# One gather in sixteen of a graph layer replaced by single-column copies on ScalarE and VectorE

## The chip, the core and the metric

The kernel runs on one core of a Trainium2 chip. The metric is device microseconds of one launch. A core has five engines that run their own instruction streams in order: TensorE (PE in the profile, with PEld its weight loads), VectorE (DVE), ScalarE (ACT), GpSimd (POOL) and SyncE (SP), which here only issues DMAs. They meet at semaphores. SBUF and PSUM are on-chip memories of 128 partitions.

## The reference

One layer of message passing on a graph of 12,500 nodes with 64 features and 200,000 edges with 32 features. The edges are sorted by their destination.

```python
msg_in = concatenate([nodes[row], nodes[col], edge_features], axis=-1)   # row = src, col = dst
messages = relu(msg_in @ mW1 + mb1) @ mW2 + mb2                          # 160 -> 128 -> 64
aggregated = segment_sum(messages, col, num_segments=12500)
upd = relu(concatenate([nodes, aggregated]) @ uW1 + ub1) @ uW2 + ub2     # 128 -> 128 -> 64
out = layernorm(nodes + upd)
```

All of it is float32. The sources of the edges are random, so `nodes[row]` is a gather; the destinations rise, so the nodes of a few hundred edges lie close together.

## The kernel before

**Splitting the first layer.** The product with mW1 is split by its three inputs. `x @ mW1[0:64]` is computed once for all nodes into a table in DRAM, `tab_a` (L422), and `x @ mW1[64:128] + mb1` into `tab_b`. An edge then needs one row of `tab_a` (by its source), one of `tab_b` (by its destination) and a product of its 32 features.

**Tiles, groups and steps.** A tile is 128 edges. SUB = 8 tiles make one step s, SUP = 16 tiles make one group g, so a group is two steps; j = s % 2 tells which. There are 1563 tiles, 98 groups and 196 steps. The main loop (L583 to L622) writes out by hand what is issued in each step, and every engine takes its instructions in that order.

**The row gather.** `gather(s)` (L153) issues eight indirect DMAs on POOL, one for each tile: 128 rows of 512 bytes of `tab_a` into one of 14 row buffers. In the first XG = 8 steps rows of x are gathered in its place, and their product is made in `node_part`. A step's gathers are issued up to 13 steps ahead; `frees` (L145) tells which add must be done for the buffer to be free: the gathers of step s + 13, issued in step s, wait for the add of step s - 1.

**The edge product.** `edge_part(s)` (L242) makes eight matmuls of contraction 64 into PSUM tile `pc`. The weights are 32 rows of edge features and 32 rows of a one-hot matrix that picks the destination (L); the other operand is 32 rows of mW1 and a window of 32 rows of `tab_b` (rhs), which SP loads at an address read from a register (`windows`, L213). It is issued one step ahead: `edge_part(s + 1)` in step s. A float32 matmul shows as two pairs of weight load and matmul in the profile.

**Add and relu.** `node_part(s)` (L255) adds the gathered rows to `pc` on DVE (L272) and applies relu on ACT (L273), for all eight tiles at once. 

**The sum over edges.** `collect(s - 1)` in step s (L283) multiplies h by a one-hot selection of 32 slots for each tile (L298) into PSUM tile `sums`, and counts edges in `cnt` (L303). The selection is made by `select(g + 1)` in the even step of group g (L183): L190, L192 and L196 on DVE. Its buffer is one of two, so L196 waits for the `collect` of step s - 1. `counts` casts it on ACT (L204), in order behind it.

**Updates.** The destinations of some groups share one `sums` tile; 54 such updates follow one another over the run, each over fewer groups as the run goes on. With `due` an odd step: in the even step before it `close` copies the sums from PSUM on ACT (L317, L318), placed at the end of the step before this change; in the due step `update` makes the second layer's input (PE, L333, L334) and its relu (ACT, L336); in the even step after that `residual` makes the output and its statistics (PE L344, L345; DVE L349, L351; ACT square root L353); one step later `norm` scales (DVE L359, L362), first on DVE before that step's add, and `store` writes out. `columns` loads the x columns of the update's nodes.

**The start.** `chunk_a` makes `tab_a` in 13 chunks, with loads and stores on ACT's DMA queue, before the main loop. `rest(s)` spreads other loads and weight preparation over the first steps.

The order in the loop is: norm, windows, node_part, collect, select and load and counts (j = 0) or loadd (j = 1), a chunk of `tab_b`, edge_part of the next step, carry, update, residual, close, columns, rest, store.

Of the kernel before, what the change touches and what calls it, by code (L numbers as in the profile page):

```python
# [10 lines left out]
F32 = mybir.dt.float32  # L11
I32 = mybir.dt.int32
AF = mybir.ActivationFunctionType
ALU = mybir.AluOpType
# [3 lines left out]
P = 128  # L18
# [22 lines left out]
EARLY = NCH * P  # L41
GE = 20
BS = 8
UB = 3
NCOL = (-(-N // P) + UB) * P
UW = UB * P
# [16 lines left out]


@with_exitstack
def gnn_kernel(ctx: ExitStack, tc: tile.TileContext, x1T, x, eT, e_rows, src, dst, dst_row, wrow, wnext, whalf,
               mW1, mb1, mW2, mb2, uW1, ub1, uW2, ub2, out):

# [33 lines left out]
    past = const.tile([1, 1], F32, name="past")  # L104
    w1b = const.tile([P, DH], F32, name="w1b")
    b1 = const.tile([P, DH], F32, name="b1")

    sums_s = [const.tile([P, UW], F32, name=f"sums_s{k}") for k in range(2)]
    xw = [const.tile([P, UW], F32, name=f"xw{k}") for k in range(2)]
# [21 lines left out]
    cps = cpool.tile([P, WIN + SUP], F32, name="cps")  # L131
    slot = cps[:, :WIN]
    drc = const.tile([P, NT], F32, name="drc")
    flag_i = const.tile([1, 1], I32, name="flag_i")
    usup = const.tile([1, K], I32, name="usup")
    ustep = const.tile([1, K], I32, name="ustep")
# [4 lines left out]

    rows = ctx.enter_context(tc.tile_pool(name="rows", bufs=ROWB))
    xg = {}

    def frees(s):  # L145

# [3 lines left out]
    def tiles(s):  # L150
        return range(s * SUB, min((s + 1) * SUB, NT))

    def gather(s):  # L153

        if s >= XG or s % 2 == 0:
            buf = rows.tile([P, SUB, DH], F32, name="xg")
        else:
            buf = xg[s - 1][0]
        if s < XG:
            a = buf.rearrange("p k (b d) -> p (k b) d", d=D)[:, s % 2 * SUB:(s % 2 + 1) * SUB, :]  # L160
        else:
            a = buf.rearrange("p (b k) d -> p k b d", b=2)
        for i, t in enumerate(tiles(s)):
            nc.gpsimd.indirect_dma_start(  # L164
                out=a[:, i, :] if s < XG else a[:, i // 2, i % 2, :], out_offset=None, in_=A[:, :] if s >= XG else x[:, :],
                in_offset=bass.IndirectOffsetOnAxis(ap=src_s[:, t:t + 1], axis=0))
        xg[s] = buf, a

    with tc.tile_pool(name="sup", bufs=2) as sup, tc.tile_pool(name="work", bufs=2) as work, tc.manual_schedule():
# [31 lines left out]
        def counts(g):  # L201
            nt = min(SUP, NT - g * SUP)
            sb = sup.tile([P, SUP, WIN], BF, name="selb")
            nc.scalar.copy(sb[:, :nt], S[g][:, :nt])  # L204
            SB[g] = sb
# [27 lines left out]
            nc.scalar.copy(xt, pt)  # L233
            xs[s] = xt

        def parts(n):

            if n == SUB:
                return [slice(0, SUB)]
            return [slice(b * SUB // 2, b * SUB // 2 + (n - b + 1) // 2) for b in range(2) if n > b]  # L240

        def edge_part(s):  # L242

            n = len(tiles(s))
            g, j = divmod(s, SUP // SUB)
            pc = psum.tile([P, 2, SUB // 2, DH], F32, name="pc")
            for i in range(n):
                k, b = divmod(i, 2)
                q, m = 64 * b, j * SUB // 2 + k

                nc.tensor.matmul(pc[:, b, k, :], L[g][q:q + 64, m, :], rhs[g % 2][q:q + 64, m, :],  # L251
                                 start=s >= XG or k == 0, stop=s >= XG)
            pcs[s] = pc

        def node_part(s):  # L255

            n = len(tiles(s))
            pc = pcs.pop(s)
            h = work.tile([P, 2, SUB // 2, DH], F32, name="h")
            if s < XG:  # L260
                xt = xs.pop(s)
                for i in range(n):
                    k, b = divmod(i, 2)
                    q = 64 * b
                    nc.tensor.matmul(pc[:, b, k, :], xt[q:q + 64, k, :], w1a[q:q + 64], start=False,
                                     stop=i + 2 >= n)
                nc.scalar.activation(h, pc, AF.Relu)
            else:
                hf, pf = (t.rearrange("p b k f -> p (b k) f") for t in (h, pc))
                a = xg.pop(s)[0]  # L270
                for m in parts(n):
                    nc.vector.tensor_tensor(hf[:, m], pf[:, m], a[:, m], op=ALU.add)  # L272
                    nc.scalar.activation(hf[:, m], hf[:, m], AF.Relu)  # L273
            hs[s] = h

        def opened(u):
# [37 lines left out]
        def close(u):  # L314

            ps, pn = sums.pop(u)
            nc.scalar.copy(sums_s[u % 2], ps)  # L317
            nc.scalar.copy(xw[u % 2][0:1], pn)  # L318

        us = {}  # L320

# [46 lines left out]
            nc.sync.dma_start(out[bass.ds(n0, UW), :].rearrange("(c p) d -> p c d", p=P), o)  # L368


        WCH = 1024

        def relative(a, b):

# [19 lines left out]
        def columns_of(c, queue):  # L394

            xl = work.tile([P, HB * P], F32, name="xl")
            for h, m in spread(c):
                o = (c + HB * h) * P
                queue.dma_start(xl[64 * h:64 * h + 64, :m * P], x1T[1:, o:o + m * P])
            xls[c] = xl  # L400
# [82 lines left out]
        for k, c in enumerate(range(0, NB, NCH)):  # L483
            chunk_a(c)
            if k == 0:
                chunk_b(0, [B0v, Bv])
            if k == 2:

                w0 = wint[:, :GE * SUP]
                nc.vector.tensor_scalar(past, w0[:, GE * SUP - 1:], float(EARLY - WIN), None, op0=ALU.is_gt)  # L490
                nc.vector.tensor_scalar(w0, w0, float(EARLY - WIN), None, op0=ALU.min)
                windows(0)
                windows(1)
            if k == 4:
                relative(0, 8 * SUP)
            if k == 6:
                offsets()
            if k == 9:
                select(0)
                load(0)  # L500
                counts(0)
        columns_of(NCH, nc.sync)

        def rest(s):

            if s == 1:
                relative(8 * SUP, 8 * SUP + WCH)
            elif s == 2:
                relative(8 * SUP + WCH, NT)
                halves(4 * SUP, NTP // 2)  # L510
            elif s == BS:
                nc.sync.dma_start(wa, wrow.rearrange("o (p c) -> (o p) c", c=SUP))
                nc.sync.dma_start(wb, wnext.rearrange("o (p c) -> (o p) c", c=SUP))
                nc.scalar.dma_start(w2, mW2)
                nc.scalar.dma_start(u1a, uW1[D:2 * D, :])
                nc.scalar.dma_start(b2c, mb2.rearrange("(f o) -> f o", o=1))
                nc.vector.memset(uz[:D], 0.0)
                nc.vector.memset(ux[:D], 0.0)
                nc.vector.memset(eps, EPS)
                nc.vector.memset(ones, 1.0)  # L520
                nc.vector.tensor_copy(ux[D:], ident[D:, D:])
                nc.scalar.dma_start(uz[D:], uW1[0:D, :])
                nc.scalar.dma_start(ux[ONE:ONE + 1], ub2.rearrange("(o f) -> o f", o=1))
                nc.scalar.dma_start(ub1_s, ub1.rearrange("(f o) -> f o", o=1))
                nc.scalar.dma_start(u2, uW2)
            elif s == BS + 2:
                weights()
                checks()
# [54 lines left out]
        for s in range(last + 3):  # L583
            g, j = divmod(s, SUP // SUB)
            while gathered < NSUB and frees(gathered) < s:
                gather(gathered)
                gathered += 1
            if s - 2 in due:
                norm(due[s - 2])
            if s + 2 < NSUB:  # L590
                windows(s + 2)
            if s < NSUB:
                node_part(s)
            if 1 <= s <= NSUB:
                collect(s - 1)
            if j == 0 and g + 1 < NSUP:
                select(g + 1)
                load(g + 1)
                counts(g + 1)
            if j == 1 and g + 2 < NSUP:  # L600
                loadd(g + 2)
            if chunks and s >= BS and chunks[0] < NCH + NB * (s + 1 - BS) / (SUP // SUB * (GE - 1) - BS):
                if len(chunks) > 1:
                    columns_of(chunks[1], nc.sync)
                chunk_b(chunks.pop(0), [Bv])
            if s + 1 < NSUB:
                if s + 1 < XG:
                    transpose(s + 1)
                edge_part(s + 1)
            if s in due and due[s] + 1 < K:  # L610
                carry(due[s] + 1)
            if s in due:
                update(due[s])
            if s - 1 in due:
                residual(due[s - 1])
            if s + 1 in due:
                close(due[s + 1])
            if s + 2 in due:
                columns(due[s + 2])
            rest(s)  # L620
            if s - 2 in due:
                store(due[s - 2])  # L622
# [166 lines left out]
```

## Time and profile before

| what | value |
|---|---|
| median of three runs | 2792.62 us (2783.0 to 2799.24) |
| profiled execution, its time and span | 2797.45 us, 2795.7 us |
| PE, PEld busy | 1650.0 us (59%), 1427.7 us (51%) |
| POOL busy | 1476.6 us (53%) |
| DVE, ACT busy | 553.1 us (20%), 361.6 us (13%) |
| mean granted TensorE clock | 0.540 |
| indirect DMAs of `tab_a` and of x | 1499 and 64, 944 ns each |
| DMA engines' share; bytes moved | 0.2 to 0.3 in the main loop; 213.70 MB |

A row of the groups' view has the line, the engine, the operation, the tiles written and read, a count, busy time and the mean duration, then the idle time before these instructions and what ended it. "issue" is a wait for nothing that the profile shows, and "remote" one for something that the profile can't name. A timeline row has the start and duration in us, and in brackets the engine's idle time before it. Issuing of DMAs and register operations on an engine's sequencer are not counted as busy. [...]

In the main loop DVE and ACT each work a few microseconds in a step:

| row | engine | count | mean ns |
|---|---|---|---|
| L272 add | DVE | 189 | 1210 |
| L273 relu | ACT | 189 | 1047 |
| L190, L192, L196 selection | DVE | 84, 84 and 84 of the middle part | 220, 1221, 688 |
| L204 cast | ACT | 98 | 616 |
| L317, L318 close | ACT | 46 each of the middle part | 463, 462 |

### The profile page before, as it was taken

How to read it: one execution, taken by the hardware profiler on the slowest of the kernel's cores; microseconds unless marked ns; L12 is line 12 of the kernel's file. 1: busy time of each engine (PE TensorE's matmuls, PEld its weight loads, DVE VectorE, ACT ScalarE, POOL GpSimd, SP SyncE). 2: the span in 40 equal slices, each digit the busy share in tenths (PEclk: the TensorE clock that was granted, in tenths of full speed). 3: DMA queues.
4: the chain of work that ended last, by engine and by line, in shares of the span. 5: the costliest groups of instructions: out<-in, count | busy, mean ns of one | idle time of the engine just before them, and what ended most of it. 6: DMA issues, size and time to landing. Idle time of an engine off the chain costs nothing. (4 is left out here: it accounts for less than half of the span.)

```text
span 2795.7 us, 34750 instructions
## 1 busy us (share of the span) xinstructions
PE 1650.0 (59%) x9558; PEld 1427.7 (51%) x9558; DVE 553.1 (20%) x1103; ACT 361.6 (13%) x534; POOL 1476.6 (53%) x1572
## 2 busy tenths in 40 slices
PE   1412755555564646655656655656666676675788
PEld 1312654555454545544546544555555555564667
DVE  0200121222111112111211211212122222221233
ACT  0100101101010111111111111111111111111122
POOL 7175445654555655555555564565555555555510
PEclk6555555555555555555555555555555555555566
DMA  3531233333222222222222222222222222222221
GB/s 89 144 90 51 74 84 91 90 93 85 69 75 67 78 67 73 74 72 72 74 73 74 73 75 71 70 77 76 71 76 66 77 75 75 75 78 73 74 69 44
DMA packets 248063, 213.70 MB, mean 76 GB/s; under 512 B 81153, under 2 KB 213143, under 8 KB 247880
## 3 DMA queue, kind: packets, MB, share of 16 engines
q0 software_dynamic: 50016, 100.44, 14.0%
q1 hardware_dynamic: 182310, 100.72, 13.1%
q10 hardware_dynamic: 15554, 10.31, 1.3%
q8 instruction: 90, 1.47, 0.2%
q14 instruction: 93, 0.76, 0.1%
HBM read 192.55 MB, written 18.68 MB: 76 GB/s over the span
## 5 line engine op out<-in xcount | busy, mean ns | idle before, releaser
L164 POOL DMA_INDIRECT xg<-tab_a,src_s x1499 | 1415.0, 944 | 1183.8 <-DVE h L272 440.6
L251 PE MATMUL pc<-rhs,l 64*128 64x128 f32 x3126 | 531.4, 424 | 677.5 <-issue 411.8
L251 PEld LDWEIGHTS pc<-rhs,l 64*128 64x128 f32 x3126 | 432.1, 306 | 733.9 <-issue 629.4
L298 PEld LDWEIGHTS sums<-sel,h 128*128 128x128 f32 x3126 | 637.2, 301 | 206.6 <-issue 199.8
L298 PE MATMUL sums<-sel,h 128*128 128x32 f32 x3126 | 626.8, 366 | 151.7 <-issue 149.8
L272 DVE TENSOR_TENSOR h<-pc,xg 128x1024 f32<-128x1024 f32 x189 | 228.6, 1210 | 954.5 <-remote 319.5
L273 ACT ACTIVATE h<-h 128x1024 f32<-128x1024 f32 x189 | 197.7, 1047 | 598.9 <-DVE h L272 495.3
L196 DVE TENSOR_TENSOR sel<-cps,drc 128x512 f32<-128x512 f32 x98 | 67.3, 686 | 634.6 <-remote 333.4
L192 DVE TENSOR_TENSOR l<-l,cps 128x1024 f32<-128x1024 int32 (+1 forms) x101 | 123.3, 1221 | 206.0 <-DMA l<-in_dst_row 159.6
L204 ACT CAST selb<-sel 128x512 bf16<-128x512 f32 x98 | 60.4, 616 | 667.4 <-DVE sel L196 398.4
L303 PE MATMUL cnt<-selb,one 128*1 128x32 bf16 x1563 | 95.2, 188 | 51.0 <-issue 50.6
L336 ACT ACTIVATE hTu<-pu,ub_s 128x384 f32<-128x384 f32 x54 | 31.3, 580 | 696.0 <-remote 308.5
L344 PE MATMUL py<-ux,xw 128*128 128x64 f32 x324 | 95.5, 384 | 26.7 <-issue 23.1
L303 PEld LDWEIGHTS <-one 128*1 128x1 bf16 x1563 | 62.7, 83 | 89.7 <-issue 77.5
L345 PE MATMUL py<-u,hTu 128*128 128x64 f32 x324 | 93.9, 382 | 21.1 <-issue 20.7
L344 PEld LDWEIGHTS py<-ux,xw 128*128 128x128 f32 x324 | 77.1, 288 | 34.3 <-issue 28.4
L345 PEld LDWEIGHTS py<-u,hTu 128*128 128x128 f32 x324 | 79.8, 297 | 26.0 <-issue 25.5
L408 PE MATMUL pb<-w1a,xl 64*128 64x128 f32 x196 | 30.6, 430 | 99.6 <-DMA xl<-in_x1T 93.2
L333 PE MATMUL pu<-sums_s,w2u 128*128 128x384 f32 x108 | 88.2, 921 | 1.5 <-ACT sums_s L317 1.5
L408 PEld LDWEIGHTS pb<-w1a,xl 64*128 64x128 f32 x196 | 26.2, 311 | 103.7 <-issue 92.8
L334 PE MATMUL pu<-xw,uz 128*128 128x384 f32 x108 | 73.7, 782 | 0.0
L349 DVE BATCH_NORM_STATS2 st<-py 128x6 f32<-128x64 f32 x162 | 26.6, 220 | 237.6 <-PE py L345 120.3
(86 smaller groups left out, 594.3 us busy)
## 6 DMA issues: line engine op xcount, KB each, us to landing
l<-in_dst_row SPq DMA_DIRECT2D x196, 128.0 KB
l<-in_eT SPq DMA_DIRECT2D x196, 128.0 KB
rhs<-tab_b SPq DMA_DIRECT2D x1563, 16.0 KB
xg<-tab_a,src_s POOLq DMA_INDIRECT x1499
tab_b<-tb SPq DMA_DIRECT2D x13, 512.0 KB
tab_a<-tb ACTq DMA_DIRECT2D x12, 512.0 KB
xw<-in_x1T SPq DMA_DIRECT2D x54, 97.5 KB
out<-o SPq DMA_DIRECT2D x54, 96.0 KB
```

The source lines that it names most:

```text
L164: nc.gpsimd.indirect_dma_start(out=a[:, i, :] if s < XG else a[:, i // 2, i % 2, :], out_offset=None, in_=A[:, :] if s >= XG else x[:, :], ...
L192: nc.vector.tensor_tensor(l[r], l[r].bitcast(I32), node[r].unsqueeze(2).broadcast_to([r.stop - r.start, SUP // 2, P]), op=ALU.is_equal)
L196: nc.vector.tensor_tensor(s[:, :nt], slot.unsqueeze(1).broadcast_to([P, nt, WIN]), drc[:, g * SUP:g * SUP + nt].unsqueeze(2).broadcast_to( ...
L251: nc.tensor.matmul(pc[:, b, k, :], L[g][q:q + 64, m, :], rhs[g % 2][q:q + 64, m, :], start=s >= XG or k == 0, stop=s >= XG)
L272: nc.vector.tensor_tensor(hf[:, m], pf[:, m], a[:, m], op=ALU.add)
L273: nc.scalar.activation(hf[:, m], hf[:, m], AF.Relu)
L298: nc.tensor.matmul(ps[:, bass.ds(ws[i], WIN)], h[:, i % 2, i // 2, :], S[g][:, k0 + i, :], start=False, stop=ends and i == n - 1)
L303: nc.tensor.matmul(pn[:, bass.ds(ws[i], WIN)], one, SB[g][:, k0 + i, :], start=False, stop=ends and i == n - 1)
L333: nc.tensor.matmul(pu, w2u, sums_s[u % 2], start=True, stop=False)
L334: nc.tensor.matmul(pu, uz, xw[u % 2], start=False, stop=True)
L344: nc.tensor.matmul(py[:, i], xw[u % 2][:, i * P:(i + 1) * P], ux, start=True, stop=False)
L345: nc.tensor.matmul(py[:, i], hT[:, i * P:(i + 1) * P], u2, start=False, stop=True)
```

## The change

For one tile of each two groups (CG = 2 here counts steps of eight tiles: every second step, the odd ones, from step 13 on, where the step is full), the last tile of the step is no longer gathered. In its place its 128 x columns are put together on chip: x, transposed, is kept whole in SBUF (`xcol`, 64 partitions by 12,544 columns, loaded by SP in seven DMAs near the end of the table's making), and in each of two steps 64 columns are copied one by one into `xo` at addresses read from registers, 36 by ACT and 28 by DVE (`copies`). DVE does it as an addition of a zero that lies in PSUM. The sources of these tiles come from a small table `srow`, whose values are loaded into registers of ACT (twice 18) and DVE (28). A further matmul in `edge_part` multiplies `xo` by the weights `w1a` and adds to the tile's part of `pc`. In `node_part` the add covers seven tiles in such steps, and the last tile has a relu of its own straight from PSUM. `copies(s)` is called in each step behind the selection and the chunk of `tab_b` and ahead of the next `edge_part`; it works for the odd step two or three ahead.

Besides, `close` moves from the step's end to right behind `collect`, ahead of the selection and its cast.

```diff
+CG = 2
+CF = 6 * CG
+CA = 36
+NCT = -(-(NSUB - CF) // CG)
...
+    xcol = const.tile([P, NB * P], F32, name="xcol")
...
+    srow = const.tile([NCT, P], I32, name="srow")
+    xo = [const.tile([P, P], F32, name=f"xo{k}") for k in range(2)]
...
+    def copied(s):
+
+        return s >= CF and s % CG == CG - 1 and len(tiles(s)) == SUB
...
-        for i, t in enumerate(tiles(s)):
+        for i, t in enumerate(tiles(s)[:SUB - copied(s)]):
...
+                c = copied(s) and i == n - 1
                 nc.tensor.matmul(pc[:, b, k, :], L[g][q:q + 64, m, :], rhs[g % 2][q:q + 64, m, :],
-                                 start=s >= XG or k == 0, stop=s >= XG)
+                                 start=s >= XG or k == 0, stop=s >= XG and not c)
+                if c:
+                    nc.tensor.matmul(pc[:, b, k, :], xo[s // CG % 2][q:q + 64], w1a[q:q + 64], start=False, stop=True)
...
-                for m in parts(n):
+                for m in parts(n, copied(s)):
                     nc.vector.tensor_tensor(hf[:, m], pf[:, m], a[:, m], op=ALU.add)
                     nc.scalar.activation(hf[:, m], hf[:, m], AF.Relu)
+                if copied(s):
+                    nc.scalar.activation(h[:, 1, SUB // 2 - 1], pc[:, 1, SUB // 2 - 1], AF.Relu)
...
+        def copies(s):
+
+            t = (s + 2) // CG * CG + CG - 1
+            if t < CF or not t < NSUB or not copied(t):
+                return
+            n = P // CG
+            k = (s + 2) % CG * n
+            r = t // CG - CF // CG
+            to = xo[t // CG % 2]
+            def by_dve(o, i):
+                nc.vector.tensor_tensor(o, i, slot[D:, 0:1], op=ALU.add)
+
+            parts = []
+            for a, b, e, copy in ((k, k + CA // 2, ET.Activation, nc.scalar.copy),
+                                  (k + CA // 2, k + CA, ET.Activation, nc.scalar.copy),
+                                  (k + CA, k + n, ET.DVE, by_dve)):
+                _, v = nc.values_load_multi_w_load_instructions(
+                    srow[r:r + 1, a:b], engines=[e], min_val=0, max_val=N - 1,
+                    skip_runtime_bounds_check_because="sources are node numbers")
+                parts += [(copy, a + i, v[i]) for i in range(b - a)]
+            for copy, i, v in parts:
+                copy(to[D:, i:i + 1], xcol[D:, bass.ds(v, 1)])
...
+        XCH = 2048
...
+        def xload(c):
+
+            e = min(c + XCH, NB * P)
+            nc.sync.dma_start(xcol[D:, c:e], x1T[1:, c:e])
...
                 select(0)
                 load(0)
                 counts(0)
+                for c in range(0, NB * P, XCH):
+                    xload(c)
...
             elif s == 2:
+                nc.sync.dma_start(srow, src_row[CF * SUB + SUB * CG - 1::SUB * CG, :][:NCT])
...
             if 1 <= s <= NSUB:
                 collect(s - 1)
+            if s + 1 in due:
+                close(due[s + 1])
             if j == 0 and g + 1 < NSUP:
                 select(g + 1)
                 load(g + 1)
...
                 chunk_b(chunks.pop(0), [Bv])
+            copies(s)
...
                 residual(due[s - 1])
-            if s + 1 in due:
-                close(due[s + 1])
```

More of the change, by code (lines that the diff above doesn't have):

```diff
@@ L65, in gnn_kernel @@
 @with_exitstack
-def gnn_kernel(ctx: ExitStack, tc: tile.TileContext, x1T, x, eT, e_rows, src, dst, dst_row, wrow, wnext, whalf,
+def gnn_kernel(ctx: ExitStack, tc: tile.TileContext, x1T, x, eT, e_rows, src, src_row, dst, dst_row, wrow, wnext, whalf,
                mW1, mb1, mW2, mb2, uW1, ub1, uW2, ub2, out):
@@ L234, in transpose, with parts @@
             xs[s] = xt
-        def parts(n):
+        def parts(n, last=False):
             if n == SUB:
-                return [slice(0, SUB)]
+                return [slice(0, SUB - last)]
             return [slice(b * SUB // 2, b * SUB // 2 + (n - b + 1) // 2) for b in range(2) if n > b]
@@ L771 @@
         "src": sp.reshape(-1, P).T[:, :NT],
+        "src_row": sp.reshape(-1, P),
         "dst": dp[:EPAD].reshape(-1, P).T[:, :NT],
```

## The prediction

> **What bounds the kernel now.** I read the page's first part, then the waits, the timeline of one stretch, then each engine's rows there. No engine is full: PE 59%, POOL 53%. The waits (who waited, for whom, us in all, times, longest) say who holds whom:
>
> ```profile
> POOL xg L164 <- issue: 442.6, 1434, 1.0
> POOL xg L164 <- DVE h L272: 440.6, 67, 16.0
> ...
> POOL xg L164 <- DVE cps L190: 223.3, 50, 11.8
> ```
>
> A gather is 944 ns and 0.30 us of issue behind it, 1.25 us; eight are 10.0 us a step. POOL is idle 664 us more (second and third line), waiting for the add of L272, whose end frees a row buffer (the L190 behind it is named where it comes later). So DVE's adds start POOL's runs. From the add of step 11 (367.9 us, from the timeline) to that of step 182 (2687.2) a step takes 13.6 us: 10.0 of gathers, the rest mostly waits for an add. What delays the adds is seen in the timeline, here DVE's, then PE's and POOL's rows:
>
> ```profile
> 1498.47 1.22 DVE L272 TENSOR_TENSOR h<-pc,xg 128x1024 f32<-128x1024 f32 x1 [5.97 <-remote]
> 1499.61 0.22 DVE L190 TENSOR_SCALAR cps<-wh,pidx 128x8 f32<-128x8 int32 x1
> 1502.74 1.22 DVE L192 TENSOR_TENSOR l<-l,cps 128x1024 f32<-128x1024 int32 x1 [2.91 <-DMA l<-in_dst_row]
> 1515.51 0.69 DVE L196 TENSOR_TENSOR sel<-cps,drc 128x512 f32<-128x512 f32 x1 [11.55 <-remote]
> 1516.12 1.22 DVE L272 TENSOR_TENSOR h<-pc,xg 128x1024 f32<-128x1024 f32 x1
> ```
>
> ```profile
> 1504.16 0.37 PE L251 MATMUL pc<-rhs,l 64*128 64x128 f32 x1 [0.35 <-issue]
> 1505.59 0.37 PE L251 MATMUL pc<-rhs,l 64*128 64x128 f32 x1 [1.06 <-issue]
> ```
>
> ```profile
> 1511.49 0.94 POOL L164 DMA_INDIRECT xg<-tab_a,src_s  x1 [0.30 <-issue]
> 1517.60 0.94 POOL L164 DMA_INDIRECT xg<-tab_a,src_s  x1 [5.16 <-DVE h L272]
> ```
>
> While the rows of a run of gathers arrive, SP starts an instruction only each 0.70 us (or a multiple; 1503.43 to 1504.13 to 1504.85 here), and so does PE, once it has run some 80 more; PE's semaphores reach DVE late. Here the run ended at 1512.4 and the slow stretch at 1515.4, when selection and add went at once; 1.5 us later POOL had its next buffer. POOL's gap is 3.0 (tail) + 0.7 (L196) + 1.2 (L272) + 0.25 = 5.2 us. **What stands on DVE between the tail's end and the add stands in POOL's path.** DVE and ACT are not slowed in these stretches by what they do there now: up to 23 DVE instructions went at 0.1 us each.
>
> **What the change takes away.** One of 16 gathers in each odd step from 13 to 193: 91 x 1.25 = **-114 us**, if the gaps stay.
>
> **What it adds.** In each step 36 one-column copies on ACT and 28 on DVE, each with a register operation in front (PE has 3232 of these for its 3126 dynamic addresses), behind register loads (TENSOR_LOAD: 0.30 us for one value, 0.59 for eight, so an estimated 1.0 for 18 and 1.4 for 28; the sequencer does them while the engine waits or works, so I put them at nothing; uncovered on DVE they would cost 1.4 a step more). The trace has no such copy. Bounds. DVE: L351's small operations start 0.075 us apart, a whole L190 takes 0.22, so 2.1 to 6.2 us a step. I take L349's spacing, 0.135 us (three in 0.49; it too reads PSUM), plus a little for the register operation: 0.15, **4.2 us**. ACT, nearest row:
>
> ```profile
> 1921.58 0.30 ACT L353 ACTIVATE sd<-mv,eps 128x3 f32<-128x3 f32 x1 [3.20 <-DVE mv L351]
> 1921.78 0.46 ACT L317 COPY sums_s<-sums 128x384 f32<-128x384 f32 x1
> ```
>
> The next starts 0.203 us after a three-column operation: **7.3 us**. [...]
>
> **Where these lie.** In an even step they stand behind the selection of the next group (L190 to L196, on ACT the cast L204), before the next step's add, and before the residual's L349 to L353. I went through the timeline for all 86 even steps from 12 to 182:
> - In 33 of them L196 ended a wait and the add followed it with nothing between (as at 1515.51). The gathers cannot cover the copies: DVE's 4.2 us go in full between L196 and the add. 33 x 4.2 = **+141**.
> - In 46 a residual follows. An example, ACT's rows and then DVE's:
>
> ```profile
> 1536.06 0.62 ACT L204 CAST selb<-sel 128x512 bf16<-128x512 f32 x1 [4.55 <-issue]
> 1543.05 0.30 ACT L353 ACTIVATE sd<-mv,eps 128x3 f32<-128x3 f32 x1 [6.37 <-DVE mv L351]
> ```
>
> ```profile
> 1542.30 0.49 DVE L349 BATCH_NORM_STATS2 st<-py 128x6 f32<-128x64 f32 x3 [6.33 <-remote]
> 1542.71 0.30 DVE L351 BATCH_NORM_AGGREGATE mv<-st 128x2 f32<-128x6 f32 x3
> 1543.38 0.18 DVE L359 RECIPROCAL rs<-sd 128x3 f32<-128x3 f32 x1 [0.36 <-ACT sd L353]
> 1543.59 0.85 DVE L362 TENSOR_SCALAR o<-py,mv,rs 128x64 f32<-128x64 f32 x3
> 1544.35 1.21 DVE L272 TENSOR_TENSOR h<-pc,xg 128x1024 f32<-128x1024 f32 x1
> ```
>
> The add waits for the square root by way of L359 and L362. It is queued on ACT behind the copies, which end 0.7 + 7.3 = 8.0 us after L196; it now starts 0.75 behind L349, and L349 on average some 4 us after L196's end. Counted step by step, 42 are late, **+134** in all. Also queued behind ACT's copies: the next relu and, in a step that is due, hTu (L336); both mostly fall in a slow stretch, in which PE gets nowhere.
> - In the other even steps and in the odd ones the copies run beside POOL's run; in 12 odd steps DVE's idle time is under 4.2: **+22**.
>
> Together **+297**. [...]
>
> **End and start.** After the last gather (2681 us) two steps take 13.7 us, with some 4.4 of ACT (25.1 us in the last 96). With 2 x 7.3 more ACT needs 19.0: +5.3 for each of five pairs still copying, **+27**. At the start 3.2 MB of x columns go through SP's queue near 125 us, when queues move 200 to 260 GB/s; tab_a's last stores, which the gathers wait for, share that: **+8** (0 to 13; were they late altogether, the long first run at 138.6 us starts later). SP's issues for them, seven at about 0.4 us, stand before the windows of step 2, which wait for that first run anyway.
>
> **One answer each.** The new matmul is four short PE instructions in two steps; it waits for copies that were queued a step or more before, so I charge nothing; uncovered it would stop PE's queue, and the add behind it. The close moved ahead of the cast saves 0.6 us of ACT order; it and the cast wait for the same sums, so nothing (without the move it would stand behind 7.3 us of copies). The add over seven tiles saves an eighth of 1.22 us in each odd step, some 0.15 x 91 = 14 us at most, and the separate relu adds about 0.3 on ACT: together nothing. srow is one small DMA.
>
> **Sum.** -114 + 297 + 27 + 8 = +218. The profiled execution took 2797.45 us (span 2795.7), 4.8 over the median of the three runs, 2792.62. From it 3015 us; against the median about 3010. I forecast **3015 us**, the copies behind blocked selections; own range 2900 to 3160, chance 0.50.
>
> **Rivals.**
> - *Hidden, faster* (0.20): the later adds give PE and SP more clear time, selections come before the slow stretch, and all copies lie beside gathers: 2797 - 114 + 27 + 8 = **2718**. For it: the 8-gather runs, in which L196 went at 1535.29. Against it: PE's collect, which L196 waits for, comes behind an add and its relu (1.2 + 1.1 + 4 us), and SP is slow 1 to 3 us after the rows begin to come. With a copy at some 0.10 us on both engines and no tail it is near 2810.
> - *Throttled sequencers, slower still* (0.20): ACT and DVE, now with over 70 instructions a step, are held to one each 0.70 us like SP. Slow stretches fill some 8.6 us of a step (1580 us of SP's rows), room for 12 instructions, six copies. ACT's other 30 (6.0 us) and its 1.8 us of other work need clear time, where a step has about 5: 8.1 + 6.0 + 1.8 = 15.9 against 13.6, +2.3 x 171 = 393, with +35 for both ends **3225**, up to 3400 with waits behind it. For it: PE and SP. Against: DVE's 23.
> - *No change* (0.03): at the low prices, +85 or +147 against 114.
> - Between the last and the forecast's range: 0.07.
>
> Within 0.5% (14 us) is what a measurement cannot tell from no change. Faster 0.20, same 0.03, slower 0.77. The range 2700 to 3360 takes in the upper part of the first rival, leaves out the far end of the second, and holds the unknown prices.
>
> **What would show it.** Right: rows of 28 DVE copies between L196 and L272 where none stood, 0.15 us apart; ACT's 0.20 apart; POOL's wait for DVE up from 664 to near 950 us while its issues fall by 91. Wrong: a POOL gap of 5 us still behind blocked selections; copies at 0.08 us; copies 0.7 us apart in the runs (the throttle); or PE's new matmul waiting long for xo, which I put at nothing. If selections stop waiting, the first rival has it.

## The result, and the profile after

The changed kernel takes 2962.77 us (median of 4 runs, 2939.45 to 2982.32) where the kernel before, run beside it, takes 2795.93: a ratio of 1.0596, 95% interval 1.0504 to 1.0687. It is slower by 167 us. A second series of the same kernel, run later, gave 3006.05 (ratio 1.0775, 1.0685 to 1.0865), so the loss is 167 to 215 us.

The profiled execution has a span of 2955.8 us (2795.7 before). Its waits, in the same columns as those of before:

```profile
ACT xo L358 <- issue: 1328.7, 949, 6.4
POOL xg L176 <- DVE h L287: 665.3, 86, 18.7
DVE xo L347 <- issue: 637.4, 871, 1.8
POOL xg L176 <- issue: 409.2, 1291, 7.5
...
PE pc L267 <- ACT xo L358: 240.1, 40, 15.9
POOL xg L176 <- DVE cps L202: 226.2, 75, 4.0
...
DVE rs L399 <- ACT sd L393: 155.0, 54, 6.5
```

POOL's waits that name DVE rise from 664 to 892 us; its issue time falls with the 91 gathers. New are PE's wait for the copied columns and, largest of all, idle time of ACT ahead of copies that nothing in the profile explains ("issue"). L399's wait for the square root is 155 us, where the same wait was 17 before. From POOL's rows I made an account of the whole span. A run is a row of gathers that follow one another after 0.30 us; a gap is a pause of over 0.6 us between two runs. The last two columns belong to experiments below.

| us | before | after | no_copies | aligned |
|---|---|---|---|---|
| up to the first gather of `tab_a` | 138.6 | 148.3 | 146.7 | 145.4 |
| in runs | 1834.5 | 1708.9 | 1720.4 | 1704.7 |
| in gaps | 708.3 | 944.0 | 644.8 | 798.0 |
| after the last gather | 114.3 | 154.6 | 116.9 | 118.9 |
| span | 2795.7 | 2955.8 | 2628.8 | 2767.1 |

The runs are 126 us shorter, and the gaps 236 us longer. (Some 14 of the 126 only changed their place: there are 46 more gaps, and each holds 0.30 us that stood in a run.) What DVE does inside the gaps, summed from its rows (what is left of the gaps is smaller work):

| us inside POOL's gaps | before | after | aligned |
|---|---|---|---|
| column copies | 0 | 115 | 75 |
| idle, then a copy | 0 | 143 | 98 |
| idle, then L399 (waits for the square root) | 13 | 127 | 52 |
| the add itself | 142 | 190 | 192 |
| idle, then the add | 183 | 144 | 162 |
| idle, then the selection L208 | 138 | 69 | 51 |
| idle, then the statistics L389 | 90 | 14 | 34 |

Of the 143 us ahead of copies 53 stand before the first copy of a step and 90 between copies. One gap of 15.7 us shows most of this. The timeline of the changed kernel, POOL's rows, then DVE's, then ACT's (start, duration, and in brackets the idle time before):

```profile
1577.40 0.94 POOL L176 DMA_INDIRECT xg<-tab_a,src_s  x1 [0.30 <-issue]
1594.05 0.94 POOL L176 DMA_INDIRECT xg<-tab_a,src_s  x1 [15.71 <-DVE h L287]
```

```profile
1580.14 0.69 DVE L208 TENSOR_TENSOR sel<-cps,drc 128x512 f32<-128x512 f32 x1 [10.38 <-remote]
1582.23 0.42 DVE L347 TENSOR_TENSOR xo<-xcol,cps 64x1 f32<-64x1 f32 x3 [1.40 <-issue]
1582.97 3.25 DVE L347 TENSOR_TENSOR xo<-xcol,cps 64x1 f32<-64x1 f32 x25 [0.32 <-issue]
1586.25 0.50 DVE L389 BATCH_NORM_STATS2 st<-py 128x6 f32<-128x64 f32 x3
1586.78 0.32 DVE L391 BATCH_NORM_AGGREGATE mv<-st 128x2 f32<-128x6 f32 x3
1591.72 0.18 DVE L399 RECIPROCAL rs<-sd 128x3 f32<-128x3 f32 x1 [4.62 <-ACT sd L393]
1591.93 0.85 DVE L402 TENSOR_SCALAR o<-py,mv,rs 128x64 f32<-128x64 f32 x3
1592.70 1.08 DVE L287 TENSOR_TENSOR h<-pc,xg 128x896 f32<-128x896 f32 x1
```

```profile
1583.21 0.61 ACT L216 CAST selb<-sel 128x512 bf16<-128x512 f32 x1
1587.37 2.92 ACT L358 COPY xo<-xcol 64x1 f32 x28 [3.55 <-issue]
1590.48 0.89 ACT L358 COPY xo<-xcol 64x1 f32 x8 [0.19 <-issue]
1591.39 0.30 ACT L393 ACTIVATE sd<-mv,eps 128x3 f32<-128x3 f32 x1
```

The 28 DVE copies stand between L208 and L287, as forecast. The square root L393 stands behind ACT's 36 copies, as forecast. But the copies of ACT take 4.0 us here, not 7.3, and 3.55 us before them ACT does nothing. DVE has 1.40 of the same. The views of line L353, where the registers are loaded, give the reason (count, then shortest, median and longest in ns):

```profile
L353 ACTq TENSOR_LOAD <-srow x364: 746/2759/5341, 355.1 to 2909.3; - x182
L353 DVEq TENSOR_LOAD <-srow x182: 1847/1896/2157, 355.2 to 2906.0; - x182
```

ACT's median mixes two kinds: in nearly every step its first load takes about 1.50 us and its second about 4.00 (medians), though both bring 18 values. In the gap above the second runs from 1583.29 to 1587.21, and the first copy starts at 1587.37. What makes the second slower is the question of the last two experiments.

The 0.70-us stretches, too, now reach the copies. ACT's rows in another step of the same timeline:

```profile
1537.17 1.84 ACT L358 COPY xo<-xcol 64x1 f32 x15 [4.57 <-issue]
...
1550.44 0.19 ACT L358 COPY xo<-xcol 64x1 f32 x1 [1.19 <-issue]
1551.18 0.19 ACT L358 COPY xo<-xcol 64x1 f32 x1 [0.55 <-issue]
1552.57 0.19 ACT L358 COPY xo<-xcol 64x1 f32 x1 [1.20 <-issue]
1553.32 0.29 ACT L358 COPY xo<-xcol 64x1 f32 x2 [0.56 <-issue]
```

```profile
1553.65 0.79 PE L267 MATMUL pc<-w1a,xo 64*128 64x128 f32 x2 [15.19 <-ACT xo L358]
```

Single copies start 0.74, 1.39 and 0.75 us apart here, and PE, whose new matmul waits for the last of them, stands for 15.19 us. In the whole run 630 of ACT's 6370 intervals from copy to copy are 0.6 us or longer (610 us in all), and 573 of DVE's 4914 (557 us).

### The profile page after: what moved, and what is told of

Its sections match the earlier page's. It is cut to its first block, busy times and chain, and to the rows that moved or that the text cites. A ratio compares the mean times of both kernels' runs of the same rounds, so it can differ in the third digit from the quotient of the medians.

```text
span 2955.8 us, 58846 instructions
## 1 busy us (share of the span) xinstructions
PE 1634.4 (55%) x9740; PEld 1417.7 (48%) x9740; DVE 1231.8 (42%) x6199; ACT 1106.8 (37%) x7177; POOL 1393.7 (47%) x1481
## 5 line engine op out<-in xcount | busy, mean ns | idle before, releaser
L176 POOL DMA_INDIRECT xg<-tab_a,src_s x1408 | 1332.0, 946 | 1386.4 <-DVE h L287 665.3
L358 ACT COPY xo<-xcol 64x1 f32 x6552 | 746.8, 188 | 1330.6 <-issue 1328.7
L347 DVE TENSOR_TENSOR xo<-xcol,cps 64x1 f32<-64x1 f32 x5096 | 684.6, 159 | 640.9 <-issue 637.4
L315 PEld LDWEIGHTS sums<-sel,h 128*128 128x128 f32 x3126 | 655.6, 313 | 171.2 <-issue 118.9
L264 PE MATMUL pc<-rhs,l 64*128 64x128 f32 x3126 | 432.7, 426 | 481.5 <-DVE o L402 171.9
L264 PEld LDWEIGHTS pc<-rhs,l 64*128 64x128 f32 x3126 | 363.3, 314 | 507.5 <-DVE o L402 189.5
L287 DVE TENSOR_TENSOR h<-pc,xg 128x1024 f32<-128x1024 f32 (+1 forms) x189 | 217.0, 1148 | 314.6 <-DMA xg<-tab_a,src_s 137.4
L288 ACT ACTIVATE h<-h 128x1024 f32<-128x1024 f32 (+1 forms) x189 | 187.9, 995 | 137.8 <-DVE h L287 132.8
L208 DVE TENSOR_TENSOR sel<-cps,drc 128x512 f32<-128x512 f32 x98 | 67.2, 685 | 385.2 <-remote 208.1
L267 PE MATMUL pc<-w1a,xo 64*128 64x128 f32 x182 | 64.3, 454 | 280.5 <-ACT xo L358 240.1
L267 PEld LDWEIGHTS pc<-w1a,xo 64*128 64x128 f32 x182 | 46.1, 311 | 303.6 <-ACT xo L358 260.8
L373 PE MATMUL pu<-sums_s,w2u 128*128 128x384 f32 x108 | 88.2, 920 | 146.7 <-DVE h L287 70.3
L373 PEld LDWEIGHTS pu<-sums_s,w2u 128*128 128x128 f32 x108 | 26.9, 309 | 156.2 <-DVE h L287 73.3
L384 PEld LDWEIGHTS py<-ux,xw 128*128 128x128 f32 x324 | 82.9, 313 | 15.7 <-ACT hTu L376 7.3
```

What stands on the lines that cost most here:

```text
L176: nc.gpsimd.indirect_dma_start(out=a[:, i, :] if s < XG else a[:, i // 2, i % 2, :], out_offset=None, in_=A[:, :] if s >= XG else x[:, :], ...
L315: nc.tensor.matmul(ps[:, bass.ds(ws[i], WIN)], h[:, i % 2, i // 2, :], S[g][:, k0 + i, :], start=False, stop=ends and i == n - 1)
L347: nc.vector.tensor_tensor(o, i, slot[D:, 0:1], op=ALU.add)
L358: copy(to[D:, i:i + 1], xcol[D:, bass.ds(v, 1)])
L373: nc.tensor.matmul(pu, w2u, sums_s[u % 2], start=True, stop=False)
L384: nc.tensor.matmul(py[:, i], xw[u % 2][:, i * P:(i + 1) * P], ux, start=True, stop=False)
```

## The experiments

Two theories stood at first. The **queue**: what stands on DVE ahead of the add, and on ACT ahead of the square root, is paid in POOL's gap. The **throttle**: ACT's added instructions fall into the 0.70-us stretches, and PE waits for `xo`. Register loads had a part in the queue theory alone: some 50 us on ACT and, taking nearly all idle time ahead of copies in the gaps for loads, 121 on DVE, where only 53 lie ahead of the first copy of a step. The first four runs take the change apart, and were made on one chip, beside a kernel before of 2789.22 us.

**No copies at all.** The gathers stay reduced, the matmul reads zeros, to which `xo` is set once at the start.

```diff
-            copies(s)
```

> The changed kernel without any copy and register load for one: xo is set to zero once, so the product of the last tile's x rows in each odd step is left out; gathers, the further matmul, the load of xcol and the moved close stay as changed. Theory Q (queue: copies and register loads stand on DVE and ACT ahead of the add that frees POOL): all of the loss goes, the gathers' gain stays, 2796 - 126 + 10 and perhaps less than 10 us of tail, 2680 to 2700 us. Theory T (throttle: copies at 0.70 us in the runs of gathers hold up PE's matmul with xo): the same 2680 to 2700. If it stays above 2760, the loss lies in something else, the matmul, the seven-tile add or xcol's load.

Measured 2623.95 us, ratio 0.9394 (0.9341 to 0.9447). The gathers and the rest of the change are worth 165 us, not 114. The account shows where the other 51 lie: the runs are 114 us shorter, the gaps 64, and start and end 11 longer. All that the copies and their loads cost is therefore some 340 us by the first series of the changed kernel, and 382 by the second, which ran on the same chip as this run. Both theories had the gain too small.

**DVE's 28 copies alone**, the other columns left at zero in the same way.

```diff
-            for a, b, e, copy in ((k, k + CA // 2, ET.Activation, nc.scalar.copy),
-                                  (k + CA // 2, k + CA, ET.Activation, nc.scalar.copy),
-                                  (k + CA, k + n, ET.DVE, by_dve)):
+            for a, b, e, copy in ((k + CA, k + n, ET.DVE, by_dve),):
```

> Only DVE's 28 copies of a step and their load; ACT's 36 columns of xo stay zero, so a part of the last tile's product is left out. Theory Q: the square root is no longer behind ACT's copies (113 us of POOL's gaps in the changed kernel), DVE's copies (115) and its register loads (121) stay: 2830 to 2870 us, with rows of 28 copies and 1.7 us of idle time ahead of them still in POOL's gaps. Theory T: ACT's copies were the ones PE waited for (240 us), so with them gone most of the loss goes: 2700 to 2760.

Measured 2779.17 us, ratio 0.9968 (0.9946 to 0.9990): DVE's part costs 155 us over no copies. The value lies between the two ranges and favours neither.

**ACT's 36 copies alone**, in two loads of 18.

```diff
-                                  (k + CA // 2, k + CA, ET.Activation, nc.scalar.copy),
-                                  (k + CA, k + n, ET.DVE, by_dve)):
+                                  (k + CA // 2, k + CA, ET.Activation, nc.scalar.copy)):
```

> Only ACT's 36 copies of a step and their two loads; DVE's 28 columns of xo stay zero, so a part of the last tile's product is left out. Theory Q: DVE's copies and loads leave POOL's gaps (236 us), the wait of the reciprocal for the square root stays (some 110 us or a little more): 2730 to 2800 us. Theory T: PE's matmul still waits for ACT's copies, 240 us in the changed kernel: 2900 to 2960.

Measured 3166.34 us, ratio 1.1343 (1.1282 to 1.1405): slower than the whole change, with less work, and past both ranges. Its waits:

```profile
ACT xo L357 <- issue: 1551.7, 1261, 6.3
POOL xg L176 <- DVE h L287: 943.0, 85, 17.6
...
PE pc L267 <- ACT xo L357: 803.0, 85, 15.5
```

PE waits for `xo` in 85 steps, not 40. The profile shows 46 runs of 15 gathers here and 5 in the changed kernel. My reading is that in the long ones ACT comes to its copies in the midst of a 0.70-us stretch and PE's queue stands until the stretch ends, and that DVE's copies, by delaying adds, break these runs and give ACT clear time; no run has that alone. The two parts don't add up in any case (155 and 542 us over no copies, and some 340 or 382 for both), and PE's wait for ACT's copies grows from 240 to 803 us. What brings ACT to its copies so late was not yet known.

**The same copies from fixed columns**: no register loads and no register operations; the columns are the wrong ones.

```diff
-                _, v = nc.values_load_multi_w_load_instructions(
...
-                copy(to[D:, i:i + 1], xcol[D:, bass.ds(v, 1)])
+                parts += [(copy, a + i, 97 * (a + i)) for i in range(b - a)]
...
+                copy(to[D:, i:i + 1], xcol[D:, v:v + 1])
```

> All 64 copies of a step, but from fixed columns of xcol (97 times the place), so without register loads and without the register operation ahead of each copy; the last tile of the odd steps gets the wrong x rows. Theory Q: copies of 0.10 and 0.13 us stay in POOL's gaps (115 us, and the square root behind ACT's 3.6 us), the loads go (121 us on DVE, some 50 on ACT): 2770 to 2830 us. Theory T: half the instructions, so the copies are done before the slow stretch bites and no copy stands 0.70 us after another; if the throttle was the loss: 2700 to 2740.

Measured 2773.33 us, ratio 0.9936 (0.9915 to 0.9958). All 64 copies are there, and 190 us of the first series are gone, 233 of the second, which ran on the same chip. This is in the queue theory's range: the way to the addresses costs more than the copies, which keep some 150 us (2773 against 2624). ACT's longest idle time ahead of a copy falls from 6.4 to 1.2 us:

```profile
ACT xo L355 <- issue: 632.1, 906, 1.2
```

The throttle is still there, with 846 of ACT's intervals at 0.6 us or longer, where its theory had expected none. Copies now start 0.072 us apart on DVE in the clear and 0.091 on ACT, instead of 0.129 and 0.101, so 0.057 of the 0.129 us of a DVE copy went with its register operation. The run doesn't tell what the loads cost from what the register operations cost.

**Three runs on a chip without the stretches.** These and a fourth for reference ran on another chip, on which the kernel before takes 1984.47 us. There the 0.70-us stretches are missing: after the first 250 us 15 of SP's intervals are near 0.70 or 1.40 us in the kernel before with a third buffer, against 1610 in the kernel before on the other chip. POOL runs from its first gather to its last almost without a gap: in the kernel before with a third buffer 1469 of its waits are issue, none over 0.3 us, 447.8 us in all. The expectations had been put in numbers for the other kind of chip, so what they were to tell apart could not be told; and the changed kernel as it is was not run on this chip.

*The copies two steps earlier*, into one of three `xo`:

```diff
-            t = (s + 2) // CG * CG + CG - 1
+            t = (s + 4) // CG * CG + CG - 1
...
-            k = (s + 2) % CG * n
+            k = (s + 4) % CG * n
```

> All copies, worked two steps earlier (for the odd step four or five ahead) into three xo tiles, so that PE's matmul with xo comes at least two steps behind its copies. Theory T (ACT's copies at 0.70 us hold up PE at this matmul, and all behind it): PE's wait for xo (240 us in the changed kernel) goes and the add comes earlier: 2780 to 2870 us. Theory Q (DVE's copies and loads, and the square root behind ACT's copies, stand ahead of the add): these stay where they are, 2930 to 2980.

Measured 2076.8 us, ratio 1.0463 (1.0446 to 1.0481). Its waits:

```profile
ACT xo L358 <- issue: 758.5, 282, 5.7
...
DVE rs L399 <- ACT sd L393: 267.2, 54, 6.7
...
POOL xg L176 <- DVE h L287: 99.6, 31, 4.2
```

POOL hardly waits, and its last gather ends at 1933 us, yet 145 us follow it (26 in the kernel before with a third buffer). ACT needs 5.5 us of loads, 3.7 of copies and some 1.8 of other work in a step, about 11, where POOL needs 9.4: the consumers fall behind the gathers and finish later. No interval from copy to copy reaches 0.6 us here, and the loads alone are half of ACT's step.

*The copies behind the residual*:

```diff
-            copies(s)
             if s + 1 < NSUB:
...
                 residual(due[s - 1])
+            copies(s)
```

> The call of the copies moved behind update and residual in each step, so the statistics (L389, L391), the square root and hTu stand ahead of the copies on DVE and ACT. Theory Q: the reciprocal's wait for the square root in POOL's gaps (127 us, before the change 13) goes and the copies of a blocked step then stand behind the statistics: 2830 to 2900 us. Theory T: copies come later still and PE waits longer for xo: 2960 to 3050.

Measured 2370.65 us, ratio 1.1952 (1.1932 to 1.1972). PE's new matmul then waits 338 us for `xo` and the gaps are 348 us, against some 100 in the run before. On this chip it is the worst of the three.

*A third buffer for the selection and its kin*, in the changed kernel and in the kernel before:

```diff
-    with tc.tile_pool(name="sup", bufs=2) as sup, tc.tile_pool(name="work", bufs=2) as work, tc.manual_schedule():
+    with tc.tile_pool(name="sup", bufs=3) as sup, tc.tile_pool(name="work", bufs=2) as work, tc.manual_schedule():
```

> The changed kernel with three buffers for the selection and its cast in place of two, so L208 does not wait for the collect of the step before. Theory Q: no selection is blocked, the copies begin right behind the add beside POOL's run: the idle time ahead of sel (69 us) and much of xo and its loads (236) leave POOL's gaps: 2780 to 2860 us. Theory T: more copies fall into the slow stretches and PE waits more for xo: 2930 to 3050.

> The kernel before with three selection buffers. A blocked selection costs there only its own 0.7 us and the cast's order: 34 x 0.7 = 24 us less, 2760 to 2795 us, under either theory; under 2740 would mean that the waits of L196 cost more than DVE's own time behind them.

Measured 2084.63 us, ratio 1.0497 (1.0479 to 1.0516), and 1984.0 us, ratio 1.0000 (0.9991 to 1.0008). To the kernel before the third buffer is worth nothing on this chip. The change with it loses 5%; what the buffer does for the changed kernel itself can't be told without that kernel's time here.

**Half of it**, beside the changed kernel itself, again on a chip with the stretches (before 2791.45 us): one tile of each four groups, 18 copies on ACT in one load and 14 on DVE.

```diff
-CG = 2
+CG = 4
...
-CA = 36
+CA = 18
```

> Half of the change: one tile of each four groups (every fourth step) instead of each two, so about 45 gathers fewer instead of 91, and 18 copies on ACT (one load of 18 values) and 14 on DVE in each step; the close stays moved. Two cases, by the chip that this run meets. On a chip with 0.70-us stretches (kernel before near 2790 us): the theory 'what stands on DVE ahead of an add and on ACT ahead of the square root is paid in POOL's gap' has -165 x 45/91 = -82 us (from the run without copies) and about half of the register loads and copies in 34 to 50 blocked steps, some +90: 2770 to 2830, ratio 0.99 to 1.015. The rival 'a fixed number of copies falls into each slow stretch, so ACT only gets slow above some 50 instructions' has ACT's series unthrottled and no wait of PE for xo: 2700 to 2760, ratio 0.97 to 0.985. On a chip without such stretches (before near 1985 us): POOL's unbroken run is the bound, so -45 x 1.25 = -56 us and, with ACT's work in a step down from about 11 to 6 us, no long tail: 1925 to 1945, ratio 0.97 to 0.98; if instead the copies delay adds as on the other chip: 1985 or more.

> The changed kernel itself, unaltered, beside the others of this call. On a chip with 0.70-us stretches (before near 2790 us): ratio 1.05 to 1.07, 2930 to 2985 us. On a chip without them (before near 1985 us): no gap of POOL from copies ahead of an add, but ACT needs about 5.5 us of register loads, 3.7 of copies and 1.8 of other work, 11 us a step, where POOL needs 9.4, so the consumers fall behind and the work after the last gather grows to over 100 us: ratio 1.04 to 1.06, 2065 to 2105 us. If ACT's register loads cost nothing there, ACT has 5.5 us a step, no long tail, and the ratio is 0.945 to 0.96.

Half the change measured 2937.21 us, ratio 1.0510 (1.0453 to 1.0568), far above what either theory allowed; the whole one 3006.05, ratio 1.0775 (1.0685 to 1.0865). Half the change has two thirds of the loss (146 of 215 us). The loads of this kernel:

```profile
L352 ACTq TENSOR_LOAD <-srow x168: 700/1474/1729, 518.0 to 2881.1; - x168
L352 DVEq TENSOR_LOAD <-srow x168: 1034/3258/4291, 521.8 to 2879.7; - x168
```

DVE loads 14 values in 3.26 us, where 28 took 1.90. Ahead of an add stand now 3.26 + 1.84 = 5.1 us, against 1.90 + 3.65 = 5.55 for twice the columns. What the slow loads have in common is where they start: ACT's second 18 values at byte 72 of a step's share of a row, DVE's 14 at byte 72; the fast ones start at byte 0 or 144. That is the third theory, of the **misaligned load**: the start decides the time, at byte 72, which is no multiple of 16, 0.22 to 0.23 us a value, at 0 and 144 0.07 to 0.08. The last two runs test it, again on a chip with the stretches (before 2792.51 us).

**The changed kernel with ACT's loads as 20 and 16**, all else as it was:

```diff
+CA1 = 20
...
-            for a, b, e, copy in ((k, k + CA // 2, ET.Activation, nc.scalar.copy),
-                                  (k + CA // 2, k + CA, ET.Activation, nc.scalar.copy),
+            for a, b, e, copy in ((k, k + CA1, ET.Activation, nc.scalar.copy),
+                                  (k + CA1, k + CA, ET.Activation, nc.scalar.copy),
```

> The changed kernel with ACT's 36 values loaded as 20 and 16 instead of 18 and 18, nothing else changed. In all runs so far a load of 18 values that starts 72 bytes into its row took 4.04 us, one of 14 values at 72 bytes 3.26, while 18 values at byte 0 took 1.51 and 28 at byte 144 took 1.9. Theory A: a load whose start is not a multiple of 16 bytes costs about 0.23 us a value, an aligned one 0.07 to 0.08; so the load of 16 at byte 80 takes 1.2 to 1.4 us, ACT is 2.5 us a step shorter, the square root behind it is as much earlier in some 50 residual steps. On a chip with 0.70-us stretches (before near 2790 us): -125 from the changed kernel, 2830 to 2890 us, ratio 1.015 to 1.035. On a chip without them (before near 1985 us): ACT's 11 us a step become 8.5, less than POOL's 9.4, so the long tail goes and the 91 gathers show: 1870 to 1910, ratio 0.94 to 0.965. Rival: the second load of a step is slow whatever its start, or ACT's copies at 0.70 us set the time: load near 4 us or no gain, ratio 1.06 to 1.08 (first kind of chip) or 1.04 to 1.05 (second).

Measured 2777.95 us (10 runs), ratio 0.9969 (0.9932 to 1.0006). Moving one boundary by two values takes 185 us from the first series of the changed kernel and 228 from the second, and the whole loss with it. The changed kernel itself was not run on this chip, but the kernel before takes the same there within 4 us. Loads, then waits, of this kernel (its lines stand one further down):

```profile
L354 ACTq TENSOR_LOAD <-srow x364: 1017/1203/1506, 350.1 to 2730.9; - x182
```

```profile
ACT xo L359 <- issue: 1075.0, 1315, 2.3
...
POOL xg L177 <- DVE h L288: 510.7, 86, 18.5
...
PE pc L268 <- ACT xo L359: 88.4, 19, 15.1
...
DVE rs L400 <- ACT sd L394: 58.1, 54, 4.4
```

The two loads take 1.29 and 1.04 us. DVE's wait for the square root falls from 155 to 58 us and PE's for `xo` from 240 to 88. The gain is larger than the 125 expected, since more than the square root moved: the tables above have 146 us less of gaps, with only 2 of over 15 us where the changed kernel had 18, and 36 less after the last gather. A step with a residual now looks like this, DVE's rows, then POOL's:

```profile
1682.63 0.49 DVE L390 BATCH_NORM_STATS2 st<-py 128x6 f32<-128x64 f32 x3 [0.90 <-PE cnt L321]
1683.16 0.31 DVE L392 BATCH_NORM_AGGREGATE mv<-st 128x2 f32<-128x6 f32 x3
1684.48 0.18 DVE L400 RECIPROCAL rs<-sd 128x3 f32<-128x3 f32 x1 [1.00 <-ACT sd L394]
```

```profile
1686.81 0.94 POOL L177 DMA_INDIRECT xg<-tab_a,src_s  x1 [6.21 <-DVE h L288]
```

The square root is 1.00 us late, not 4.62, and the gap is 6.2 us, not 15.7. The throttle is still there: 1002 of ACT's intervals from copy to copy are 0.6 us or longer, *more* than the 630 of the changed kernel. So their number doesn't tell the loss. What part they have in the 154 us by which this kernel stays above the one without copies is open.

**Half of it with ACT 20 and DVE 12**, so that DVE's load starts at byte 80:

```diff
-CA = 18
+CA = 20
```

> The kernel with one tile of each four groups, split 20 on ACT and 12 on DVE instead of 18 and 14, so that DVE's load starts at byte 80 of its quarter instead of 72. Theory A: DVE's load of 3.26 us becomes 0.8 to 1.1 and two copies (0.26) go; 2.4 to 2.7 us less ahead of the add in the 50 to 60 gaps that hold DVE's copies (281 us of load and copies in POOL's gaps at 5.1 us each). On a chip with 0.70-us stretches: -120 to -165 from the half kernel's 2937, 2770 to 2820 us, ratio 0.99 to 1.01. On a chip without them: 1920 to 1945, ratio 0.965 to 0.98. Rival: the alignment of the load is not the cause of half's loss: ratio 1.04 to 1.06 on the first kind of chip.

Measured 2824.67 us, ratio 1.0114 (1.0037 to 1.0190).

```profile
L352 DVEq TENSOR_LOAD <-srow x168: 340/860/2041, 523.1 to 2779.3; - x168
```

The load falls from 3.26 to 0.86 us and the kernel by 112, a little less than expected and far from the rival's 1.04 to 1.06; the half kernel, too, had run on another chip that has the stretches. DVE's copies and the idle time before them in POOL's gaps fall from 301 to 100 us, but idle time ahead of the statistics and of the add grows from 105 to 229: with the load gone another wait is often next. Why half the change is no better than all of it, both aligned, stays open.

No version that computes the layer beat the kernel before: the aligned one cannot be told from it on a chip with the stretches. On one without them, where POOL is the bound and ACT's step would fall from 11 to an estimated 7.8 us (loads of 2.3 in place of 5.5), the aligned one wasn't run.

## Why the prediction came out as it did

It forecast 3015 us; measured were 2963 and 3006. The sign, the mechanism of the queue and the total were right. The total is right in part by luck: an ACT copy priced at twice its time stood in for a register load priced at nothing.

- **The gathers, -114.** Without copies the runs shortened by just that, 114 us. But the change then gains 165: the gaps were not constant, as the forecast had assumed with "if the gaps stay".
- **DVE's copies ahead of the add, +141.** Right in place, and near in size: 0.129 us a copy in the clear, 3.65 a step against 4.2, and 115 us of them inside gaps. (33 x 4.2 is 139, not 141.) The reason given was wrong: a copy alone, though it too reads PSUM, takes 0.072 (the fixed columns), and the other 0.057 go with the register operation, for which "a little" was added. That L349's 0.135 came so near was luck.
- **The square root behind ACT's copies, +134.** Right in place; the idle time ahead of L399 in the gaps grew by 114 us. Wrong in its make-up. I took 0.203 us for an ACT copy, from the operation behind a three-column one; measured is 0.101, and 0.091 from the fixed columns. ACT's 36 copies are 3.7 us in the clear. What filled the place of the other 3.6 us is the load.
- **The register loads at nothing.** This is the step that failed. The forecast had estimated 1.0 us for 18 values and put it at nothing, as on PE in the kernel before, where 129.8 of the 136.0 us of 250 loads lie under PE's own matmuls and weight loads. ACT's two took 1.50 and 4.00, and the engine stood for them: 3.55 us in the example. DVE's 28 took 1.90, not 1.4, and stood uncovered there for 1.40. With ACT's second load aligned the kernel lies within 5 us of the one without any loads (2778 and 2773, ratios 0.9969 and 0.9936, on two chips). So in the total the charge of nothing would about have held for aligned loads; the misaligned one was worth 185 to 228 us, by the series of the changed kernel that is taken.
- **What the copies cost without that load.** Aligned, the whole change is 154 us over no copies, where the forecast had counted +297 and +27. Against a kernel whose loads really cost next to nothing it was thus 237 us too high (3015 and 2778).
- **The throttle.** I gave it 0.20 as a rival. Copies at 0.70 us and PE's wait for `xo`, which I had put at nothing, both came. PE's wait is large where ACT works alone (803 us) and smaller in the change (240), and most of that went with the misaligned load (88). On DVE 90 us of POOL's gaps are idle time between copies, and 60 with the load aligned.
- **No change at the low prices (0.03).** The rival set +85 or +147 against 114 and left out the start and the end; with the start's 8 us the sums are -21 and +41, both outside 14 us. No run shows a term of +85 or +147; what the runs showed in its place is 154 us over no copies with the load aligned, and some 340 or 382 as the change stood.
- **Start and end, +8 and +27.** Measured +9.7 and +40. The end's excess is the load again: aligned it is +4.6.
- **The move of the close, at nothing.** No run has it alone; it stays open.

## What to carry to other kernels

Look at the durations of register loads themselves, which no busy share counts; here lists that start at byte 0, 80 or 144 took 0.06 to 0.08 us a value, and those that start at byte 72 0.22 and 0.23. When many small operations are added to an engine, ask what stands ahead of the first of them as well as how long each one is. And a forecast whose total is right should still be taken apart: here two kernels with equal amounts of work, one boundary moved by two values, differ by 185 us, more than the 114 that the change was meant to bring.

## What the runs showed of the hardware

- **Register loads.** Median durations of single loads (us), by number of values and start byte in a step's share:

| values, start | measured | us a value |
|---|---|---|
| 18 at 0 (ACT) | 1.50 | 0.083 |
| 18 at 72 (ACT) | 4.00 | 0.222 |
| 20 at 0, 16 at 80 (ACT) | 1.29, 1.04 | 0.065, 0.065 |
| 28 at 144 (DVE) | 1.90 | 0.068 |
| 14 at 72 (DVE) | 3.26 | 0.233 |
| 12 at 80 (DVE) | 0.86 | 0.072 |
| 1 and 8 (PE, kernel before) | 0.30, 0.59 | 0.30, 0.074 |

  The last column is the second by the number of values. Of the starts on ACT and DVE 72 was slow, and 0, 80 and 144 were fast. Lists of other starts were not run, and why a load from 72 takes longer is not shown. At byte 0, 18 values took 0.21 us more than 20.
- **The 0.70-us stretches reach ACT and DVE.** In the kernel before they had shown on SP and PE alone (1610 of SP's intervals; PE's matmuls and weight loads 0.70 us or a multiple apart from 1504.16 to 1515.41, within 0.03); on DVE they showed as a wait alone: the last matmul of the collect ahead of L196 ended at 1499.67 in PE's rows, and L196 started at 1515.51. With 36 copies on ACT and 28 on DVE, each with a register operation, 149 and 143 of 182 series of copies hold an interval of 0.6 us or longer; with 18 and 14 (half of it) 88 and 9 of 168. Without register operations (fixed columns) it is 126 and 40 of 182. So the shares were lower in the runs with fewer instructions; none of the runs shows a limit.
- **They were missing on one chip.** Of the three chips that the experiments met, one did not show them, and there the kernel before takes 1984 us, not 2790, at much the same granted clock (medians of 0.556 and 0.545). These runs met that chip once, and why it differed is not known from them.
